# Layer 2 of a four-layer graph kernel: x2 turned by VectorE in squares of 32, h in x2's place, a seventh stream buffer, and the last output block stored in two parts

## The chip, the cores and the metric

The kernel runs on one core of one Trainium2 chip. The metric is the device time of one execution in microseconds (us). The core has five engines that matter here: TensorE (PE, with its weight loads PEld), VectorE (DVE), ScalarE (ACT), GpSimd (POOL) and SyncE (SP), which issues most transfers. Each engine works through its own instructions in order and waits at semaphores for the others. The core's 16 DMA engines serve the queues of SP and of ACT.

## The reference

Four layers work on x (3327 nodes, 64 features) and one dense 3327 x 3327 adjacency matrix that is mostly zeros. Each layer adds its result to its input and normalises the rows.

```python
x = _layernorm(x + _L0_gnn_ref(t, x, adj))          # elementwise after the norm
x = _layernorm(x + _L1_gnn_ref(x, adj, att_W, att_b)) # attention over all pairs of nodes
x = _layernorm(x + _L2_gnn_ref(x, adj, W))          # two hops, below
x = _layernorm(x + _L3_gnn_ref(x, adj, weight, bias)) # ranked neighbours, weights 0.5**k

def _L2_gnn_ref(user_embs, adj, W):
    x = user_embs
    for k in range(2):
        agg = adj @ x
        x = tanh(concat([agg, x], axis=1) @ W[k])
    return x
```

The change is in layer 2 and in the very end of layer 3. Layer 2 is, per hop, `tanh(adj @ (x @ W_top) + x @ W_bottom)`: the kernel multiplies by W first and then by the matrix.

## The kernel before

**Data.** The nodes are padded to 3328, which are 26 blocks of 128. The host hands in the transposed matrix, so that block `jb` of it is a tile [128, 3328] of float32: 1664 KB, or 13 KB in each partition. Four blocks (`kept`, loaded in layer 1) and two more (`late`, loaded near its end) stay in on-chip memory through layer 2. Features of nodes are kept in two forms: by node (128 nodes in the partitions, 64 features in a row) and stacked (64 features of the lower half of the nodes and 64 of the upper half in the 128 partitions, 1664 columns).

**Layer 2.** The function `layers` begins with it. `x2`, by node, is layer 1's result; the last DVE instructions of layer 1 write it (L1556 to L1558). `hT` is x2 in stacked form. It lies in the tile that the code calls `x3` or `x2T`, and since x2 + layer 2's result is formed later in stacked form (`with_x2`), it has to stay. For each of the two hops `k`:

- `top(i)` makes x @ W_top by node in `hw` (the tile `lj`), 128 nodes at a time. For hop 0 layer 1's end has made it already (`begun_here` is true in this run), so hop 0 can start with the large products.
- `bottom(c)` adds x @ W_bottom of a quarter (chunk) `c` of 416 columns to the accumulator `acc[c]` and needs `hT`. The four accumulators lie in two PSUM tiles: chunks 0 and 2 share one, chunks 1 and 3 the other.
- `add(c, jb)` adds one block's product to a chunk, for both halves of the nodes. A block takes 16 matmul records at L403.
- `chunk_end(c)` adds the last kept blocks (`end`, two in hop 0, three in hop 1) to one chunk and applies tanh on ACT. The result goes to `nxt`.

Both hops go through all 26 blocks. Hop 0 uses the six kept blocks, four blocks that were loaded ahead into the pool `strm` (four buffers), and sixteen that are loaded in the loop: into `strm`, or into the pool `more` (two buffers). The blocks loaded last in hop 0, six of them, are still there when hop 1 begins; hop 1 uses them first, and loads the other 14. SP issues a load when the buffer's former block has been used by PE (L209).

`hT` is made while hop 0 runs: after the fourth and fifth block, `turned(i)` transposes 13 groups of 128 nodes on PE (L345) into PSUM, and ACT copies them out (L349). After the sixth block come the four `bottom` products (L394), and behind the copies a one-element tanh (`warm_t`, L486) whose only purpose is that ACT loads the table of tanh.

`nxt` comes from a pool `cols` with two buffers of 6.5 KB in each partition. The same pool gives `accT` in layer 3, the sums of one half of the nodes.

**Layer 3.** When both blocks of `more` that hop 1 loaded have been used, that pool is closed and the first masks of layer 3 are made in its place (`masks`, L337). Then the layer runs through the matrix in two halves of 1664 columns, with its own half-blocks `ah` streamed in (L335). The order of PE, ACT and DVE is written out by hand in `layers` (`manual_schedule`).

**The end.** `last_out` makes the second half's output. The sums are multiplied back to nodes in three parts (blocks 0 to 5, 6 to 9, 10 to 12), x3 is added, ACT squares, DVE sums, and `rsqrt_of` gives one over the root of the variance: a step on DVE (L542), Sqrt on ACT (L236), then a reciprocal, and one refining step in four DVE instructions (L239 to L243). Each part is multiplied by it (L824) and stored, in turn by SP, ACT and SP (L764). The last block has only 127 real nodes; ACT stores it by itself (L828). After that every engine branches to the program's closing block, in which SP waits for all transfers.

Of the kernel before, what the change touches and what calls it, by code (L numbers as in the profile page):

```python
# [10 lines left out]
F32 = mybir.dt.float32  # L11
# [3 lines left out]
AF = mybir.ActivationFunctionType  # L15
ALU = mybir.AluOpType
# [3 lines left out]
P = 128  # L20
N = 3327
NB = 26
NP = NB * P
D = 64
CW = 416
HALF = NP // 2
NBH = NB // 2
# [12 lines left out]
EARLY = 4  # L40
LATE = 2
UNDER_WAY = 4

LN_EPS = 1e-5
MIN_NORM = 1e-15
# [28 lines left out]
def kernel(  # L74
# [11 lines left out]
    nc = tc.nc  # L86

    const = ctx.enter_context(tc.tile_pool(name="const", bufs=1))
    small = ctx.enter_context(tc.tile_pool(name="small", bufs=2))
# [22 lines left out]
    )  # L112
    ones = const.tile([P, 1], F32, name="ones")
    nc.vector.memset(ones, 1.0)

    attw_dg = const.tile([P, 4], F32, name="attw_dg")
    nc.vector.memset(attw_dg, 0.0)
# [147 lines left out]
    def by_half(v):  # L265

        return v.rearrange("p (n h) d -> p n h d", h=2)
# [39 lines left out]

    @with_exitstack
    def layers(ctx, x2, x3, begun_here, kept, ready, ahead_ctx, strm):
        cols = ctx.enter_context(tc.tile_pool(name="cols", bufs=2, reuse_waits="tile"))  # L310

        more_ctx = ExitStack()
        more = more_ctx.enter_context(tc.tile_pool(name="more", bufs=2, reuse_waits="tile"))
        l3m = None
        in_order = ctx.enter_context(ExitStack())
        in_order.enter_context(tc.manual_schedule(engines={mybir.EngineType.PE}))
# [20 lines left out]
            nc.vector.tensor_scalar(mask[q], at, 0.0, None, ALU.not_equal)  # L337

        groups = fours

        def to_stack(ps, src, dst, g, n, copy, name):

# [34 lines left out]
        with tc.tile_pool(name="l2p", bufs=2, space=PSUM, reuse_waits="tile") as l2p:  # L377
            for k in range(2):
                hw = lj
                nxt = cols.tile([P, HALF], F32, tag="hT", name=f"hT_{k + 1}")  # L380
                begun = set()

                def turned(i):
                    to_stack(l2p, x2, hT, *groups[i], nc.scalar.copy, "x2")

                groups = fours if k else threes

                def top(i, copy=nc.vector.tensor_copy):
                    g, n = groups[i]
                    pn = node_products(l2p, hT, w2_dg[:, 2 * k, :], g, n, f"l2_{k}")  # L390
                    copy(by_half(hw)[:, g : g + n], pn)  # L391

                def bottom(c):
                    nc.tensor.matmul(  # L394
                        acc[c], w2_dg[:, 2 * k + 1, :], hT[:, c * CW : (c + 1) * CW],
                        start=c not in begun, stop=False, skip_group_check=True,
                    )
                    begun.add(c)

                def add(c, jb, last=False):  # L400
                    for h in range(2):
                        o = h * HALF + c * CW
                        nc.tensor.matmul(  # L403
                            acc[c][h * D : (h + 1) * D, :], hw[:, slot(jb), :],
                            blocks[jb][:, o : o + CW], start=c not in begun, stop=last,
                            skip_group_check=True,
                        )
                    begun.add(c)

                stay = list(kept)
                if k:
                    stay.sort(key=lambda jb: jb >= NB - EARLY)
                n_end = 3 if k else 2
                stay, end = stay[:-n_end], stay[-n_end:]
                others = [jb for jb in range(NB) if jb not in kept and jb not in ready]
                share = -(-len(others) // len(stay))
                order = list(ready)  # L420
                if k:

                    order, others, share = order + others[:5], others[5:], 3
                for i, jb in enumerate(stay):
                    order += [jb] + others[i * share : (i + 1) * share]
                blocks = {**ready, **kept}

                if k == 0 and not begun_here:
                    turned(0)
                    turned(1)  # L430
                    top(0, nc.scalar.copy)
                    turned(2)
                    top(1)
                    for c in range(CPH):
                        add(c, order[0])
                    turned(3)
                    top(2)
                    turned(4)
                    top(3)
                    for c in range(CPH):  # L440
                        add(c, order[1])
                    top(4)
                    for c in range(CPH):
                        bottom(c)

                    warm_t = small.tile([P, 1], F32, tag="warm", name="warm_t")
                    nc.scalar.activation(warm_t, ones, AF.Tanh)
                    order = order[2:]
                elif k:
                    top(0)  # L450
                    bottom(0)
                    bottom(1)
                    top(1)
                    bottom(2)
                    for c in range(CPH - 1):
                        add(c, order[0])
                    top(2)
                    bottom(CPH - 1)
                    add(CPH - 1, order[0])
                    top(3)  # L460
                    order = order[1:]
                seen, held = {}, {}
                for i, jb in enumerate(order):
                    if jb not in blocks:
                        if len(seen) % (UNDER_WAY + 2) < 2 and (k == 0 or len(seen) < 2):
                            blocks[jb] = held[jb] = block(more, jb, tag="bt", name=f"bt_l2_{k}_{jb}")
                        else:
                            blocks[jb] = block(strm, jb, tag="at", name=f"at_l2_{k}_{jb}")
                        seen[jb] = blocks[jb]
                    for c in range(CPH):  # L470
                        add(c, jb)
                    if k == 0 and begun_here:

                        if i == 3:
                            turned(0)
                            turned(1)
                        if i == 4:
                            turned(2)
                            turned(3)
                            turned(4)  # L480
                        if i == 5:
                            for c in range(CPH):
                                bottom(c)

                            warm_t = small.tile([P, 1], F32, tag="warm", name="warm_t")
                            nc.scalar.activation(warm_t, ones, AF.Tanh)  # L486
                    if k and jb in held and len(held) == 2:
                        for q in range(AHEAD + 3):
                            masks(q)
                def chunk_end(c):  # L490
                    for jb in end:
                        add(c, jb, jb == end[-1])
                    nc.scalar.activation(nxt[:, c * CW : (c + 1) * CW], acc[c], AF.Tanh)  # L493

                if k:
                    break
                for c in range(CPH):
                    chunk_end(c)

                last = sorted(list(seen)[-UNDER_WAY - 2 :], key=lambda jb: jb not in held)  # L500
                ready = {jb: seen[jb] for jb in last}
                hT = nxt

# [36 lines left out]
        def rsqrt_of(v, w):  # L540

            nc.vector.tensor_scalar(v, v, 1.0 / D, LN_EPS, ALU.mult, ALU.add)  # L542
            return rsqrt(v, "ln", w)

        def spread(v, n):
            return v.unsqueeze(2).to_broadcast([P, n, D])
# [184 lines left out]

        def sums_out(h):

            accT = cols.tile([P, HALF], F32, tag="hT", name=f"accT_{h}")
            to = [
                accT[:, 2 * c * CW : 2 * (c + 1) * CW].rearrange("p (e k) -> p e k", e=2)
                for c in range(2)
            ]
            nc.scalar.activation(to[0], acc[h, 0], AF.Identity, bias=b3_sb)
            nc.vector.tensor_scalar(to[1], acc[h, 1], b3_sb, None, ALU.add)  # L740
            return accT
# [54 lines left out]
        def last_out(h, accT):  # L796
# [20 lines left out]
            added(2)  # L817
            summed(1)
            summed(2)
            r = rsqrt_of(v, NBH)  # L820

            rows = N - h * HALF - (NBH - 1) * P
            for s, queue in zip(parts, (nc.sync, nc.scalar, nc.sync)):
                nc.vector.tensor_tensor(  # L824
                    hh[:, s], hh[:, s], spread(r[:, s], s.stop - s.start), ALU.mult
                )
                if store(queue, h, hh, s):
                    nc.scalar.dma_start(out[N - rows :], hh[:rows, NBH - 1])  # L828

        first_out = None  # L830
        with_step = [
# [993 lines left out]
```

## Time and profile before

| what | value |
|---|---|
| median of 3 runs | 562.38 us (562.27 to 563.3) |
| the profiled execution, device time | 562.28 us |
| its span in the profile | 560.5 us |
| mean granted TensorE clock | 0.987 |
| PE busy | 527.3 us, 94% of the span |
| DVE, ACT, POOL busy | 368.2, 278.1, 215.7 us |
| layer 1 ends, first block of layer 2 on PE | 241.86 us |
| first tanh of hop 0 on ACT | 316.56 us |
| first `top` of hop 1 on PE | 320.63 us |
| first tanh of hop 1 on ACT | 396.30 us |
| last instruction issued for the output (ACT's store of 127 rows) | 554.71 us, for 0.59 us |

The span is what the profiler sees between the first and the last instruction. The device time of the same execution is 1.8 us longer. The page's 40 slices give the engines' busy tenths and what the DMA moved:

```profile
PE   8989989999999999999999999998989999999992
DVE  6899999999999999791000011300478878787834
ACT  4899999999999998612000100000274333343311
DMA  8976766676766715699999149996609996789701
GB/s 305 353 273 205 234 209 204 222 233 199 238 205 223 235 32 222 272 425 425 425 426 424 43 148 417 425 425 291 244 8 343 342 303 227 237 258 358 274 2 36
```

A slice is 14 us. Layer 2 is slices 18 to 29. There PE is busy throughout, DVE and ACT hardly at all, and the DMA moves 425 GB/s, but for two slices in the middle and two at the end. The page's list of transfers gives their sizes and the median time from issue to landing:

```profile
at_l<-in_adjT SPq DMA_DIRECT2D x26, 1664.0 KB, 13.7
bt_l<-in_adjT SPq DMA_DIRECT2D x8, 1664.0 KB, 12.8
```

`at_l` are blocks in `strm`, `bt_l` blocks in `more`: 34 loads of layer 2, of which four are those loaded ahead.

### The profile page before, as it was taken

The page shows a single profiled execution, that of the slowest core. Times are in us where ns is not written, and L with a number is a line of the kernel's source. Part 1 is how long each engine was busy: PE and PEld are TensorE (multiplying, and loading weights), DVE is VectorE, ACT ScalarE, POOL GpSimd, SP SyncE. Part 2 cuts the span into 40 slices and gives each one's busy share as a digit, 9 for nine tenths or more (in the row PEclk, how much of TensorE's full clock was granted, in tenths as well). Part 3 has the DMA queues.
Part 4 walks back from the last instruction along what each step waited for, and adds up shares of the span by engine and source line. Part 5 has one row for each costly group of instructions (what it writes and reads, how often), then busy time and mean ns, then how long its engine had stood idle before and what let it go on. Part 6 is the DMA issues. An engine that isn't in the chain of part 4 may idle for free.

```text
span 560.5 us, 7513 instructions
## 1 busy us (share of the span) xinstructions
PE 527.3 (94%) x2854; PEld 226.6 (40%) x2854; DVE 368.2 (66%) x532; ACT 278.1 (50%) x328; POOL 215.7 (38%) x138
## 2 busy tenths in 40 slices
PE   8989989999999999999999999998989999999992
PEld 5522222222222222854444444443455555545542
DVE  6899999999999999791000011300478878787834
ACT  4899999999999998612000100000274333343311
POOL 3799999999999999200000000000011000000000
PEclk9899999999999999899999999999999999999997
DMA  8976766676766715699999149996609996789701
GB/s 305 353 273 205 234 209 204 222 233 199 238 205 223 235 32 222 272 425 425 425 426 424 43 148 417 425 425 291 244 8 343 342 303 227 237 258 358 274 2 36
DMA packets 34037, 145.27 MB, mean 259 GB/s; under 512 B 10285, under 2 KB 11975, under 8 KB 28871
## 3 DMA queue, kind: packets, MB, share of 16 engines
q1 hardware_dynamic: 31655, 144.11, 69.8%
q10 hardware_dynamic: 2336, 0.59, 0.5%
q8 instruction: 24, 0.39, 0.3%
q14 instruction: 22, 0.18, 0.1%
HBM read 143.23 MB, written 0.87 MB: 257 GB/s over the span
## 4 chain that ended last, share of the span: by engine, by line
PE 61%; DVE 20%; ACT 8%; DMA 6%; issue 3%; DVEq 0%
PE cnt L403 20%; PE pq L1075 12%; DVE v L1096 12%; PE cnt L513 11%; PE acc L709 6%; DMA at_l<-in_adjT 5%; ACT sg L1051 4%; PE acc L724 3%; ACT pq L1088 3%; DVE a L1087 2%; DVE w L526 1%; PE cnt L394 1%; DVE mask L337 1%; DMA x<-in_x 1%; PE pm L1367 1%
## 5 line engine op out<-in xcount | busy, mean ns | idle before, releaser
L1062 POOL TENSOR_TENSOR u<-sg,at 128x832 f32<-128x832 f32 x88 | 170.0, 1964 | 3.5 <-ACT sg L1051 3.0
L1075 PE MATMUL pq<-riT,ljT 64*128 64x416 f32 x416 | 100.2, 560 | 15.2 <-DVE v L1096 6.2
L1087 DVE SCALAR_TENSOR_TENSOR a<-pq,dl,u 128x832 f32<-128x832 f32 x104 | 111.9, 1077 | 2.9 <-PE pq L1075 2.8
L1088 ACT ACTIVATE pq<-pq,al,gas 128x832 f32<-128x832 f32 x104 | 105.0, 1011 | 15.1 <-DVE a L1087 14.2
L1096 DVE SCALAR_TENSOR_TENSOR v<-pq,a 128x832 f32<-128x832 f32 x104 | 105.7, 1016 | 1.1 <-ACT pq L1088 0.8
L1108 PE MATMUL acc<-v,xv 128*64 128x416 f32 x416 | 95.4, 537 | 0.1
L403 PE MATMUL cnt<-at_l,lj 128*64 128x416 f32 x480 | 86.1, 513 | 2.3 <-DMA at_l<-in_adjT 2.3
L1051 ACT ACTIVATE sg<-lb,rb 128x1664 f32<-128x1664 f32 (+1 forms) x53 | 87.3, 1647 | 0.1
L528 ACT ACTIVATE w<-cnt 128x832 int16<-128x832 f32 x55 | 47.3, 863 | 71.5 <-PE cnt L513 71.4
L640 POOL TENSOR_TENSOR s<-sq,s 128x384 bf16<-128x384 f32 (+1 forms) x4 | 4.1, 1028 | 200.3 <-ACT s L639 200.3
L493 ACT ACTIVATE hT<-cnt 128x416 f32<-128x416 f32 x8 | 4.1, 517 | 138.3 <-PE cnt L403 138.3
L1075 PEld LDWEIGHTS pq<-riT,ljT 64*128 64x128 f32 x416 | 31.5, 184 | 88.3 <-DVE v L1096 83.1
L526 DVE TENSOR_SCALAR w<-cnt 128x832 int16<-128x832 f32 x49 | 50.1, 1023 | 25.8 <-PE cnt L513 24.5
L403 PEld LDWEIGHTS cnt<-at_l,lj 128*64 128x64 f32 x480 | 34.1, 137 | 52.1 <-issue 47.3
L513 PE MATMUL cnt<-mask,tri 128*128 128x416 bf16 x208 | 53.5, 339 | 0.1
L709 PE MATMUL acc<-w,s 128*128 128x416 bf16 x208 | 52.6, 339 | 0.5 <-DVE hid L781 0.5
L513 PE MATMUL cnt<-mask,rest 128*128 128x416 bf16 x200 | 51.6, 340 | 1.2 <-ACT w L528 0.6
L391 DVE COPY lj<-pn_l 128x512 f32<-128x512 f32 (+1 forms) x4 | 2.4, 592 | 73.9 <-PE pn_l L355 73.9
L1108 PEld LDWEIGHTS acc<-v,xv 128*64 128x64 f32 x416 | 20.6, 134 | 61.0 <-issue 57.8
L337 DVE TENSOR_SCALAR mask<-ah 128x1664 bf16<-128x1664 f32 x42 | 43.4, 1034 | 0.0
L403 PE MATMUL cnt<-kept,lj 128*64 128x416 f32 x192 | 35.5, 514 | 0.0
L1062 POOL TENSOR_TENSOR u<-sg,kept 128x832 f32<-128x832 f32 x16 | 31.0, 1972 | 2.6 <-ACT sg L1051 2.6
(282 smaller groups left out, 403.7 us busy)
## 6 DMA issues: line engine op xcount, KB each, us to landing
at_l<-in_adjT SPq DMA_DIRECT2D x26, 1664.0 KB, 13.7
at<-in_adjT SPq DMA_DIRECT2D x44, 832.0 KB, 4.9
ah<-in_adjT SPq DMA_DIRECT2D x42, 832.0 KB, 6.3
bt_l<-in_adjT SPq DMA_DIRECT2D x8, 1664.0 KB, 12.8
kept<-in_adjT SPq DMA_DIRECT2D x6, 1664.0 KB, 8.7
lb<-lf_rows SPq DMA_DIRECT2D x2, 384.0 KB, 4.5
ljT<-ljT SPq DMA_DIRECT2D x4, 128.0 KB, 6.2
x<-in_x ACTq DMA_DIRECT2D x1, 416.0 KB, 5.5
```

What stands on the lines that cost most here:

```text
L337: nc.vector.tensor_scalar(mask[q], at, 0.0, None, ALU.not_equal)
L403: nc.tensor.matmul(acc[c][h * D : (h + 1) * D, :], hw[:, slot(jb), :], blocks[jb][:, o : o + CW], start=c not in begun, stop=last, skip_gr ...
L513: nc.tensor.matmul(cnt[c][:, e, :], mat, mask[q][:, of], start=start, stop=(mat is tri), skip_group_check=True,)
L526: nc.vector.tensor_scalar(w.bitcast(I16), cnt[c], 0.0, None, ALU.max)
L709: nc.tensor.matmul(acc[h, c][:, e, :], s12[:, slot(jb)].rearrange("p t d -> p (t d)"), ws[q, c][:, e, :], start=first, stop=last,)
L1051: nc.scalar.activation(sg[:, :, of], lbs[:, :, of], AF.Sigmoid, bias=rb[:, sl : sl + 1])
L1062: nc.gpsimd.tensor_tensor(u, sg[:, :, of], at[:, :, of], ALU.mult)
L1075: nc.tensor.matmul(pq[:, h, :], ljT[h != jb // NBH][rows, of], riT[rows, ch * CW : (ch + 1) * CW], start=True, stop=True,)
L1087: stt(a_s[t], pqs[t], dl[:, one], us.pop(t), op0=ALU.add, op1=ALU.mult)
L1088: nc.scalar.activation(pqs[t], pqs[t], AF.Square, bias=al[:, one], scale=gas[:, one])
L1096: stt(w, pqs.pop(t), CUBIC_REST, a_s.pop(t), op0=ALU.add, op1=ALU.mult)
L1108: nc.tensor.matmul(accs[cp, ci][h * D : (h + 1) * D, :], xv[:, slot(jb), :], w[:, h, :], start=(jb == orders[cp][0]), stop=(jb == orders[c ...
```

## The change

- `cols` is no pool any more, but the tile x2 under another shape. h of both hops and both `accT` are written there. x2 has been turned into `hT` by then.
- `more` has three buffers (`MORE = 3`). With the four of `strm` there are seven; the last seven blocks loaded in hop 0 stay for hop 1, and the masks start when the third block of `more` has been used in hop 1.
- `turned_by_squares` makes `hT` by 16 DVE transposes in squares of 32 x 32, each over 13 blocks of nodes (StreamTranspose of 32x13x32), before the loop of hop 0. PE's transposes and ACT's copies in that hop go. `bottom` and `warm_t` come after the ninth block instead of the sixth.
- In `last_out`, ACT takes the Sqrt with scale and bias from the summed squares themselves; `eps` is a small tile for the bias, set by POOL at the start. The refining step has one instruction fewer, and its factor -0.5 goes into the last product.
- The 127 rows of the last block are stored as 112 (ACT) and 15 (SP).

```diff
+MORE = 3
...
+    eps = const.tile([P, 1], F32, name="eps")
+    nc.gpsimd.memset(eps, LN_EPS)
...
     def layers(ctx, x2, x3, begun_here, kept, ready, ahead_ctx, strm):
-        cols = ctx.enter_context(tc.tile_pool(name="cols", bufs=2, reuse_waits="tile"))
+
+        cols = x2.rearrange("p n d -> p (n d)")
 
         more_ctx = ExitStack()
-        more = more_ctx.enter_context(tc.tile_pool(name="more", bufs=2, reuse_waits="tile"))
+        more = more_ctx.enter_context(tc.tile_pool(name="more", bufs=MORE, reuse_waits="tile"))
...
+        def turned_by_squares(src, dst):
+
+            Q = 32
+            to = dst.rearrange("p (n k) -> p n k", k=P)
+            for h in range(2):
+                for f in range(D // Q):
+                    rows = slice(h * D + f * Q, h * D + (f + 1) * Q)
+                    for q in range(P // Q):
+                        nodes = slice(q * Q, (q + 1) * Q)
+                        nc.vector.transpose(
+                            out=to[rows, :, nodes],
+                            in_=by_half(src)[nodes, :, h, f * Q : (f + 1) * Q],
+                        )
...
-                nxt = cols.tile([P, HALF], F32, tag="hT", name=f"hT_{k + 1}")
+                nxt = cols
...
+                elif k == 0:
+                    turned_by_squares(x2, hT)
                 elif k:
...
-                        if len(seen) % (UNDER_WAY + 2) < 2 and (k == 0 or len(seen) < 2):
+                        if len(seen) % (UNDER_WAY + MORE) < MORE and (k == 0 or len(seen) < MORE):
...
-                        if i == 3:
-                            turned(0)
-                            turned(1)
-                        if i == 4:
-                            turned(2)
-                            turned(3)
-                            turned(4)
-                        if i == 5:
+                        if i == 8:
                             for c in range(CPH):
                                 bottom(c)
...
-                    if k and jb in held and len(held) == 2:
+                    if k and jb in held and len(held) == MORE:
...
-                last = sorted(list(seen)[-UNDER_WAY - 2 :], key=lambda jb: jb not in held)
+                last = sorted(list(seen)[-UNDER_WAY - MORE :], key=lambda jb: jb not in held)
...
-            accT = cols.tile([P, HALF], F32, tag="hT", name=f"accT_{h}")
+            accT = cols
...
-            r = rsqrt_of(v, NBH)
+
+            r0, r = (small.tile([P, NBH], F32, tag=f"last_{k}", name=f"last_{k}") for k in range(2))
+            nc.scalar.activation(r0, v, AF.Sqrt, bias=eps, scale=1.0 / D)
+            nc.vector.tensor_scalar(v, v, 1.0 / D, LN_EPS, ALU.mult, ALU.add)
+            nc.vector.reciprocal(r0, r0)
+            nc.vector.tensor_tensor(r, v, r0, ALU.mult)
+            nc.vector.tensor_tensor(r, r, r0, ALU.mult)
+            nc.vector.scalar_tensor_tensor(r, r, -3.0, r0, op0=ALU.add, op1=ALU.mult)
...
-                nc.vector.tensor_tensor(
-                    hh[:, s], hh[:, s], spread(r[:, s], s.stop - s.start), ALU.mult
+                nc.vector.scalar_tensor_tensor(
+                    hh[:, s], hh[:, s], -0.5, spread(r[:, s], s.stop - s.start),
+                    op0=ALU.mult, op1=ALU.mult,
                 )
                 if store(queue, h, hh, s):
-                    nc.scalar.dma_start(out[N - rows :], hh[:rows, NBH - 1])
+                    most = rows // 16 * 16
+                    nc.scalar.dma_start(out[N - rows : N - rows + most], hh[:most, NBH - 1])
+                    nc.sync.dma_start(out[N - rows + most :], hh[most:rows, NBH - 1])
```

## The prediction

> **What bounds the kernel now.** I read the chain of waits first, then the windows of layer 2, then the timeline of single engines where the chain changes hands. Line numbers are those of the kernel before; "us" are microseconds from the start of the span.
>
> The chain's shares say TensorE (PE) almost everywhere, so an edit on another engine counts only where PE, or the end, waits for it:
>
> ```profile
> PE 61%; DVE 20%; ACT 8%; DMA 6%; issue 3%; DVEq 0%
> ```
>
> The chain in order of time, cut to layer 2, shows two transfers in it, one at the end of each hop (k=0 and k=1):
>
> ```profile
> 264.31 30.90 PE cnt L403 x176
> 295.23 16.83 DMA at_l<-in_adjT
> 312.10 8.60 PE cnt L403 x48
> ...
> 330.08 47.66 PE cnt L403 x272
> 377.76 13.34 DMA at_l<-in_adjT
> 391.15 7.20 PE cnt L403 x40
> ```
>
> The windows (PE, PEld, DVE, ACT, POOL busy, granted clock, DMA share, GB/s) tell how far each of the two is from its bound:
>
> ```profile
> 228.00:300.00 72.00, 71.76 (x432) 37.87 (x432) 23.48 (x92) 11.41 (x30) 0.00 (x0) 0.98 1.00 417
> 300.00:309.00 9.00, 9.00 (x56) 3.66 (x54) 0.00 (x0) 0.00 (x0) 0.00 (x0) 1.00 1.00 423
> 309.00:312.00 3.00, 2.95 (x18) 0.99 (x14) 0.00 (x0) 0.00 (x0) 0.00 (x0) 1.00 0.25 107
> 312.00:328.00 16.00, 15.90 (x91) 8.02 (x92) 1.38 (x2) 2.07 (x4) 0.00 (x0) 1.00 0.00 1
> ...
> 388.00:391.00 3.00, 1.00 (x6) 0.14 (x2) 0.00 (x0) 0.00 (x0) 0.00 (x0) 1.00 0.07 31
> ...
> 556.80:559.20 2.40, 0.00 (x0) 0.00 (x0) 0.00 (x0) 0.00 (x0) 0.00 (x0) 0.50 0.10 24
> ```
>
> Hop 0: the DMA is full from 228 to 309 while PE is full too; both end together. Then 16 us without a transfer, because every stream buffer holds a block that hop 1 uses again. Hop 1: PE stands still before its last streamed block. The end: 2.4 us at 0.10 of the engines, a store that crawls. PE and ACT at these places:
>
> ```profile
> 253.18 0.87 PE L345 MATMUL pt_x<-ident,x 128*128 128x128 f32 x6
> 256.93 0.87 PE L345 MATMUL pt_x<-ident,x 128*128 128x128 f32 x6
> 391.15 3.01 PE L403 MATMUL cnt<-at_l,lj 128*64 128x416 f32 x16 [2.15 <-DMA at_l<-in_adjT]
> ```
>
> ```profile
> 258.70 1.28 ACT L486 ACT_TABLE_LOAD   x1
> 316.56 0.52 ACT L493 ACTIVATE hT<-cnt 128x416 f32<-128x416 f32 x1 [56.37 <-PE cnt L403]
> ```
>
> **What the Trainium skill says.** "DMA: Bandwidth & Descriptors", section "Why a DMA increments its semaphore by 16 and not by 1": a transfer from SP or ACT uses the largest number of engines up to 16 that divides the row count; 127 partitions get one engine. The trace agrees (0.10 of 16 engines above). "Vector Engine (DVE) Microarchitecture Reference", section 3.8: the 32x32 transpose sustains one element per cycle per lane; no run here shows one yet. "ScalarE: Activation LUTs", section "What ACT_TABLE_LOAD costs": 1283 ns, plus about 1380 ns of drain; the trace shows the 1.28 us and the next ACTIVATE right behind it (258.70 to 259.99), so I use 1.30. "Runtime: NRT & Kernel Launch", section "Instruction fetch mechanics": a taken branch breaks the prefetch. The trace agrees: ACT's last store is issued by 555.30 and its first record behind the branch, a drain, stands at 558.5.
>
> **1. x2 turned by DVE.** Removed: 13 PE transposes and 5 ACT copies. In PE's time that is 253.99-253.18=0.81 plus 258.31-256.93=1.38, so 2.19 us. Added: 16 StreamTranspose of 32x13x32, in DVE's queue right behind the last product of x2 (ends 254.17). The nearest row is L573, 128x416 f32 in 0.59 us; at the page's rate the transpose moves 416 elements per lane as well, so I take 0.5 to 0.6 us: 16 x 0.55 = 8.8, done at 263. PE needs it for the four "bottom" products, now behind nine blocks: 253.18 + 5 x 2.80 = 267.2. DVE has nothing else until 321.8, so nothing is queued behind. Cover is 4 us; it holds up to 0.8 us an instruction. At the low bound (0.45) nothing changes; at a high bound of 1.0 (array filled, then drained: two passes) the bottoms start at 270.2; from there 2.99 + 14 blocks x 2.80 lead to 312.4 for the last streamed block, 0.3 late, since the waits counted next absorb the rest.
>
> The 2.19 us are not gained. The last streamed block of hop 0 lands at 312.10 and the blocks land 4.0 us apart (1.704 MB at 425 GB/s), a stream that starts at 227.62 as before and carries the same 20 blocks. PE's new schedule with 2.80 us a block (264.24 to 308.98 is 16 blocks) wants block 15 at 295.3, which lands at 296.1; wants block 18 at 307.3, lands 308.1; wants the last at 310.9, lands 312.1. So PE waits 0.8+0.8+1.2 instead of computing: gain 0. DMA order and issue don't hurt: the third new buffer's first load waits for near_end's small DVE and ACT results (240.1) and sits behind two issues at 242.07, well before the queue runs dry at 248.
>
> **2. Tanh table.** With the copies gone, `warm_t` has nothing ahead of it on ACT and the order listing puts it at the start of layer 1, before the sigmoids, where ACT idles for 1.7 us (13.46 to 15.16): free, but useless as a warm-up. The load now stands directly before hop 0's first tanh and behind an event wait for that chunk's matmuls. So tanh 0 ends at 316.56+1.30+0.52=318.38 instead of 317.08. PE's matmuls for chunk 2 share chunk 0's accumulator tile and wait for tanh 0; they started at 317.74. Loss: 318.38+0.05-317.74=0.69, with restart 0.75. Tanh 1 (318.9) is needed at 319.8, so it costs once. Bounds: 0 if the load runs ahead of the wait, 2.1 if the page's drain comes on top.
>
> **3. Seventh buffer, h in x2's place.** Two `cols` tiles (2 x 6.5 KB a partition) become the third `more` block. Seven blocks stay for hop 1, so 13 are loaded instead of 14. Hop 1's first load again waits for the first reused block, 0.75 later; one block fewer is 4.0 earlier: the last lands at 391.15+0.75-4.0=387.9. PE, without stalls, wants its last streamed block (again behind 22 others) at 389.0+0.75=389.75. The 2.15 us stall goes, with 1.85 to spare; what is late next is nothing before layer 3, where all moves together. Checked on the way: each later load's buffer (four in rotation) comes free 0.4 us or more before the stream needs it. `ah`, the masks (now after the third held block, about 356, wanted at 403) and both accT in x2's place wait for things long done. Layer 2 net: -2.15+0.75=-1.40.
>
> **4. The end.** Root: before, from the variance at 551.74 to the first product at 553.30, 1.56. After, Sqrt with scale and bias runs first (0.25), `tensor_scalar` waits for it since it overwrites v (0.10 to the next issue), reciprocal 0.27, three steps of 0.21: 1.25. Gain 0.31. The products change from tensor_tensor to scalar_tensor_tensor: L613 shows 0.55 for the same 384 elements, no change. Store: 127 rows become 112 (16 engines) and 15. SP then sets the end, not the store. SP's last issue ends at 554.99 and the trace's records of its closing waits begin at 558.33, come every 0.065, then stop until 559.50 for the 127 rows; its drain is at 559.62. After: 554.99-0.31+0.45 for one more issue (stores took 0.39 to 0.59) =555.13, +3.34, + 8 x 0.065 = 558.99. The 15 rows, issued at 554.7, have landed by about 557.2. Gain 0.63 with the root in it. Bounds: 0.3 and 1.1. The `eps` memset on POOL lies in an idle stretch until 5.62: 0.
>
> **Sum.** -1.40-0.63=-2.03 on a profiled execution of 562.28 (span 560.5): 560.25. The median of the runs, 562.38, is 0.1 higher; I say 560.2.
>
> **Rivals.** (a) The table load costs nothing: 562.28-2.15-0.63=559.5. For it: ACT idles 56 us before. Against: the order listing has the wait first. (b) The last transfer's lag grows (it landed 1.5 us later than the 4.0 us step from its forerunner) or hop 1's start slips, so the stall stays: 562.28+0.75-0.63=562.4, no change. Against: 1.85 us of slack. (c) Slower: the squares. Their end, 254.2+16T, may slip to 269.9 (312.1-42.2) before the last streamed block is late, so T decides from 0.98 us and adds 16(T-0.98). At 1.5 us: 560.2+8.3=568.5. For it: no record of this instruction, strided 32-wide rows, float32. Against: the page's rate.
>
> **Numbers.** Forecast 0.64, (a) 0.14, (b) with its halfway forms 0.12, (c) 0.10. A measurement here tells 0.2% (1.1 us) from no change, so half of (b) counts as faster and half as the same. The range 559.0 to 561.4 leaves out (c) and the worse half of (b). Faster 0.83, same 0.08, slower 0.09.
>
> **What would show it.** Hop 0: PE's last streamed block still starts at 312.1, with stalls of about 0.8, 0.8 and 1.2 before it; a table load at 316.6 and chunk 2 at 318.4. Hop 1: no DMA stall, last streamed block at 389.7. End: DMA done by 557.5. Wrong if the squares end after 270, if block 19 of hop 0 starts earlier than 311.5, or if a stall remains at the end of hop 1.

## The result: 0.23% slower

| | before | changed |
|---|---|---|
| median of 20 runs each | 561.99 us (560.17 to 563.32) | 563.56 us (561.7 to 564.27) |
| ratio to before, 95% interval | | 1.0023 (1.0013 to 1.0032) |
| the profiled execution, device time (span) | 562.28 us (560.5) | 563.86 us (562.1) |

I forecast 560.2 us, a gain of about 2. It became a loss: 1.3 us by the ratio, 1.6 by the two medians.

### The profile after

The shares of the chain of waits are those of before within a point:

```profile
PE 62%; DVE 20%; ACT 8%; DMA 5%; issue 3%; DVEq 0%; ACTq 0%
```

The windows of the changed kernel (PE, PEld, DVE, ACT, POOL busy, granted clock, DMA share, GB/s):

```profile
309.00:312.00 3.00, 2.40 (x14) 0.92 (x14) 0.00 (x0) 0.00 (x0) 0.00 (x0) 1.00 0.78 328
312.00:328.00 16.00, 14.50 (x82) 6.63 (x80) 1.38 (x2) 3.24 (x5) 0.00 (x0) 1.00 0.01 5
388.00:391.00 3.00, 3.00 (x20) 1.26 (x18) 0.00 (x0) 0.00 (x0) 0.00 (x0) 1.00 0.61 252
556.80:559.20 2.40, 0.00 (x0) 0.00 (x0) 0.00 (x0) 0.00 (x0) 0.00 (x0) 0.50 0.05 11
559.20:562.00 2.80, 0.00 (x0) 0.00 (x0) 0.00 (x0) 0.00 (x0) 0.00 (x0) 0.50 0.03 9
```

Layer 2 looks as forecast: PE waits a little at the end of hop 0, and no longer in hop 1 (3.00 busy of 3.00 where it was 1.00). The last row is the news: after 559.2 no engine computes, hardly a byte moves, and still the kernel runs on to 562.1. The timeline of TensorE, VectorE and ScalarE at the places of steps 1 to 3:

```profile
256.13 10.11 DVE L354 STREAM_TRANSPOSE xc<-x 32x416 f32<-32x416 f32 x16
297.88 3.01 PE L421 MATMUL cnt<-at_l,lj 128*64 128x416 f32 x16 [0.45 <-DMA at_l<-in_adjT]
309.87 3.02 PE L421 MATMUL cnt<-bt_l,lj 128*64 128x416 f32 x16 [0.60 <-DMA bt_l<-in_adjT]
313.84 3.02 PE L421 MATMUL cnt<-bt_l,lj 128*64 128x416 f32 x16 [0.96 <-DMA bt_l<-in_adjT]
318.33 1.28 ACT L506 ACT_TABLE_LOAD   x1 [75.87 <-PE cnt L421]
320.20 3.01 PE L421 MATMUL cnt<-kept,lj 128*64 128x416 f32 x16 [0.55 <-ACT x L506]
```

The squares take 10.11/16 = 0.63 us each. Three DMA waits (0.45, 0.60, 0.96) stand in hop 0, the table load stands behind PE's products, and PE loses 0.55 us to it.

Now the end. When the stores are issued, SP runs a closing sequence of 13 instructions, all on the program's last line; the first eight are waits. The first two lines are those waits in the kernel before, in the windows 558.0 to 558.75 and 559.45 to 559.72; the next two are the changed kernel's, 558.0 to 558.95 and 560.80 to 561.34. Between the two windows of each kernel SP has no record. Columns: count, shortest/median/longest ns, first and last start.

```profile
L1821 SPq EVENT_SEMAPHORE  x6: 28/28/28, 558.3 to 558.7; - x6
L1821 SPq EVENT_SEMAPHORE  x2: 28/28/28, 559.5 to 559.6; - x2
```

```profile
L1844 SPq EVENT_SEMAPHORE  x2: 27/28/28, 558.8 to 558.9; - x2
L1844 SPq EVENT_SEMAPHORE  x6: 28/28/28, 560.9 to 561.2; - x6
```

Before: six waits 0.065 apart, then a pause that ends when the store of 127 rows lands (559.48 in the transfer records). Changed: two waits, then 2.0 us of nothing, then six in a row. The last landing was at 559.06, and no transfer arrives at 560.88, so this is no wait for data. The trace has packets of 8192 bytes at 559.34 and 560.05 in the queue that brings instructions. That alone proves little, since the kernel before, without the stop, has two such packets as well (558.93 and 559.15).

### One table for all profiles

Three stretches matter. "Start": ACT's third table load, which ends layer 1's attention. "Layer 2": from there to the first product of layer 3 on PE (`both`, L580 before). "End": from the last `accT` bias on ACT to the end of the span. Layer 3 between them takes 148.0 us in every profile.

| kernel | start | layer 2 | end |
|---|---|---|---|
| before | 234.55 | 163.73 | 14.17 |
| before_again | 234.30 | 162.46 | 13.83 |
| changed | 236.48 | 161.84 | 15.83 |
| after_again | 235.07 | 161.76 | 15.58 |
| before_pad | 236.51 | 162.59 | 15.23 |
| end_only | 236.35 | 162.43 | 13.56 |
| l2_only | 235.97 | 161.53 | 15.35 |
| after_pad2 | 236.22 | 161.65 | 13.91 |
| old_store | 236.33 | 161.80 | 13.77 |
| six_buffers | 234.92 | 162.53 | 13.54 |
| pe_turn | 235.03 | 160.89 | 13.55 |
| warm_tied | 234.83 | 160.91 | 13.73 |
| joined | 234.81 | 161.55 | 13.20 |
| joined_warm | 236.56 | 160.97 | 13.46 |

Of the 14 starts, seven lie at 234.3 to 235.1 and seven at 236.0 to 236.6. In the second group TensorE's clock stood at half for 6.8 us (12.4 to 19.8 in the records), in the first for 3.4. Before_pad runs exactly before's instructions there and is in the second group, after_again in the first, so a late start is nothing that only the changed kernel has, and the 1.9 us by which its first profile started later are not counted as its work. Whether the change makes late starts more frequent was not tested.

### The profile page after: what moved, and what is told of

The parts are those of the page before. It is cut to its first block, busy times and chain, and to the rows that moved or that the text cites. A ratio compares the mean times of both kernels' runs of the same rounds, so it can differ in the third digit from the quotient of the medians.

```text
span 562.1 us, 7490 instructions
## 1 busy us (share of the span) xinstructions
PE 526.6 (94%) x2841; PEld 226.2 (40%) x2841; DVE 377.5 (67%) x547; ACT 276.3 (49%) x323; POOL 215.6 (38%) x139
## 4 chain that ended last, share of the span: by engine, by line
PE 62%; DVE 20%; ACT 8%; DMA 5%; issue 3%; DVEq 0%; ACTq 0%
PE cnt L421 22%; PE pq L1098 12%; DVE v L1119 12%; PE cnt L526 11%; PE acc L722 6%; DMA bt_l<-in_adjT 4%; ACT sg L1074 4%; PE acc L737 3%; ACT pq L1111 3%; DVE a L1110 2%; DVE w L539 1%; PE cnt L412 1%; DVE mask L341 1%; DMA x<-in_x 1%; PE x_w L1434 1%
## 5 line engine op out<-in xcount | busy, mean ns | idle before, releaser
L421 PE MATMUL cnt<-at_l,lj 128*64 128x416 f32 x416 | 74.6, 513 | 0.5 <-DMA at_l<-in_adjT 0.5
L421 PEld LDWEIGHTS cnt<-at_l,lj 128*64 128x64 f32 x416 | 29.7, 137 | 43.2 <-issue 41.1
L506 ACT ACTIVATE x<-cnt 128x416 f32<-128x416 f32 x8 | 4.0, 516 | 79.1 <-PE cnt L421 79.0
L421 PE MATMUL cnt<-bt_l,lj 128*64 128x416 f32 x224 | 40.9, 514 | 1.6 <-DMA bt_l<-in_adjT 1.6
L506 ACT ACT_TABLE_LOAD x1 | 1.3, 1283 | 75.9 <-PE cnt L421 75.9
```

What stands on the lines that cost most here:

```text
L421: nc.tensor.matmul(acc[c][h * D : (h + 1) * D, :], hw[:, slot(jb), :], blocks[jb][:, o : o + CW], start=c not in begun, stop=last, skip_gr ...
```

## Experiments

In the "Theory F" texts, F is instruction fetch, E the end's edits themselves, S a start made later by the change. Times are medians of 9 to 22 runs (one run each for the two repeats), ratios those to the kernel before on the same chip. The experiments ran on four chips, so between experiments the ratios compare better than the medians. Each experiment but before_pad, end_only and the repeats starts from the changed kernel.

### Where SP's closing sequence lies

The kernel has an If with two arms, of which one runs. I counted SP's instructions in each built program, from 0 and with both arms (this is not in the profile). The closing sequence of 13 begins at number 849 before and at 847 in the changed kernel; in both cases SP comes to it by the branch over the arm that does not run.

**after_pad2**: the changed kernel, its closing sequence moved to 850.

```diff
+                pad = small.tile([P, 1], F32, tag="pad", name="pad")
+                for _ in range(2):
+                    nc.sync.dma_start(pad[:D, :], b3.rearrange("(d o) -> d o", o=1))
```

> The changed kernel with two small DMAs (three SP instructions) added to the arm of the If that does not run. Theory F (instruction fetch): in the changed kernel SP's closing sequence of 13 instructions stood still for 2.0 us between its second and third wait (558.86 to 560.88) because its first two instructions lie in one fetched stretch of code and the other eleven in the next; the added instructions move the whole sequence into one stretch, so the gap goes, the closing waits follow one another at 0.065 us until the last store's landing (559.1), and the time falls by 1.6 us from 563.56 to about 561.9. Theory E (the end edits themselves are slower: SP's extra store and its later branch): nothing moves, 563.5.

560.9 us, ratio 0.9987 (0.9979 to 0.9995). Two DMAs that never run turn the loss into a gain: 1.0023 against 0.9987 is 0.36%, 2.0 us (2.7 by the medians), more than the 1.6 that I expected. SP's waits of this kernel, 557.9 to 558.64:

```profile
L1847 SPq EVENT_SEMAPHORE  x8: 28/28/28, 558.0 to 558.5; - x8
```

All eight in one run, no gap. Theory E falls: what runs is the same, and the position of the code alone decides. That the stop is a fetch of instructions (theory F) is the reading that foretold it; the trace has no record that ties the stop to one fetch.

Without the gap SP is no longer the last. Its second drain comes at 558.67, ScalarE's first closing record, a drain, only at 558.92, and all engines go on at 559.17:

```profile
L1847 SPq DRAIN  x3: 7/7/13, 558.6 to 559.3; - x3
L1847 ACTq DRAIN  x2: 8/44/81, 558.9 to 559.3; - x2
```

**before_pad**: the kernel before with the same lines, 119 instead of 2, in the same arm; the closing sequence then begins at 975 = 847 + 128.

> The kernel before, with a loop of 119 small DMAs (126 SP instructions) in the arm of the If that does not run, so that SP's closing sequence begins two instructions ahead of the end of a fetched stretch if such a stretch is 128 instructions, as in the changed kernel. Nothing that runs is altered. Theory F: a gap of 2.0 us after the second closing wait, SP done at about 560.7 in place of 559.7: 1.0 us slower, 563.0. Theories E and S: no change, 562.0.

563.59 us, ratio 1.0029 (1.0016 to 1.0041). Its closing waits, 558.9 to 559.2 and 561.05 to 561.5:

```profile
L1824 SPq EVENT_SEMAPHORE  x2: 28/28/28, 559.1 to 559.1; - x2
L1824 SPq EVENT_SEMAPHORE  x6: 28/28/28, 561.1 to 561.4; - x6
```

The gap of the changed kernel appears in the old one. It was expected to cost 1.0, and in the profile the end is 1.1 to 1.4 longer than before's; the ratio says 1.6 (0.9 to 2.3).

**end_only**: the kernel before with the new root and the split store, nothing else. Closing sequence at 851.

> The kernel before with the new end alone (the shorter root and the store in 112 and 15 rows); layer 2 as before. Theory F: SP's closing sequence lies in one stretch here, so the end gains 0.24 us from the root and about 0.4 from the store that lands earlier: 561.4, no gap of 2 us among SP's closing waits. Theory E: the end costs 1.65 us as in the profiled pair, 563.6. Theory S (the later start of layer 1's attention, +1.9 us in the profiled pair, is caused by the change): if the memset of eps is its cause the start shows here too, 563 to 563.5 under F; if not, the first layer-2 block stays near 241.9.

561.96 us, ratio 1.0002 (0.999 to 1.0015). No gap among the waits; the end is 0.3 to 0.6 shorter than before's two. The time does not show this gain (561.4 was expected), but its interval, -0.6 to +0.8 us, leaves room for it. E's loss of 1.65 us is excluded. The start was late, 236.35, as in before_pad without `eps`: a late start does not need the memset.

**l2_only**: the changed kernel with the old end. Closing sequence at 845.

> The changed kernel with the old end (old root, one store of 127 rows): layer 2's part alone. Layer 2 itself should be 1.9 us shorter than before (156.4 to 154.5) in every theory. Theory F: SP's closing sequence begins four instructions ahead of the end of a fetched stretch, so a gap of 2.0 us is expected between its fourth and fifth wait, which costs 1.2 us against before, since before waited until 559.5 for the store: 562.0 - 1.9 + 1.2 = 561.3 if the start of layer 1 is chance. Theory E: the old end is as good as before, 560.1. Theory S (the warming tanh in layer 1 or the moved code makes layer 1 end 1.5 to 1.9 us later): add that, 562.9 under F.

561.94 us, ratio 0.9999 (0.999 to 1.0008). Its closing waits, 557.2 to 557.72 and 559.70 to 560.0:

```profile
L1832 SPq EVENT_SEMAPHORE  x4: 28/28/28, 557.5 to 557.7; - x4
L1832 SPq EVENT_SEMAPHORE  x4: 28/28/28, 559.7 to 559.9; - x4
```

Four waits, gap of 2.0, four waits, as expected: 845 + 4 = 849. So layer 2's gain was eaten by the position of code that layer 2 doesn't touch. The time forecast, 561.3, was 0.6 too low; the expected layer 2 gain of 1.9 came from a profile pair that overstates it (see before_again).

The positions agree on one rule: the gap comes where instruction 849 or 977 is crossed soon after the branch (after 2, 2 and 4 instructions), and none comes where the sequence starts at 849, 850, 851, 856 or 861.

### Layer 2, part by part

The next kernels all have the closing sequence in one stretch, by the same lines in the arm that does not run (two DMAs; three in old_store, eight in the two joined kernels), so after_pad2 is what they are read against.

**warm_tied**: the warming tanh can't run ahead into layer 1.

```diff
-                            nc.scalar.activation(warm_t, ones, AF.Tanh)
+                            nc.scalar.activation(warm_t, hT[:, 0:1], AF.Tanh)
```

> As after_pad2, but the warming tanh reads h's first column, so that it can't run ahead into layer 1 and the tanh table is loaded in hop 0, under TensorE's work, as before. Theory P (TensorE's own waits are the path in layer 2): the wait of 0.55 us of chunk 2 on the tanh of chunk 0 goes and the time falls by as much against after_pad2, 560.9 to 560.3. Theory D (the loads of hop 1 set layer 2's end: in after_pad2 the last streamed block landed at 390.64 and was multiplied from about 391.0): only the 0.3 us of slack can be won, 560.6, and a wait for the last streamed block appears. If the table load cost nothing, 560.9.

560.43 us, ratio 0.9972 (0.9958 to 0.9986). ACT's timeline:

```profile
240.84 1.28 ACT L499 ACT_TABLE_LOAD   x1
262.73 0.20 ACT L499 ACTIVATE warm_t<-xc 128x1 f32<-128x1 f32 x1 [20.60 <-DVE xc L354]
316.54 0.52 ACT L506 ACTIVATE x<-cnt 128x416 f32<-128x416 f32 x1 [53.60 <-PE cnt L421]
```

The table load is back under TensorE's work, PE's wait for the tanh is gone and layer 2 is 0.74 shorter (161.65 to 160.91). Theory P; the loads of hop 1 did not come in the way. Against after_pad2 the time fell by 0.5 in medians and 0.8 in ratios.

**pe_turn**: x2 turned by TensorE and ScalarE as before, all else as in after_pad2.

```diff
-                elif k == 0:
-                    turned_by_squares(x2, hT)
...
-                        if i == 8:
+                        if i == 3:
+                            turned(0)
+                            turned(1)
+                        if i == 4:
+                            turned(2)
+                            turned(3)
+                            turned(4)
+                        if i == 5:
```

> As after_pad2, but x2 is turned by TensorE with ScalarE's copies, at the same places as before, and the warming tanh stands after them. Prediction's step 1: hop 0 is bound by its loads, TensorE's 2.19 us of transposes fill time that it would otherwise wait, so hop 0's last streamed block is multiplied at the same distance from layer 2's start; and the table load comes back to hop 0, -0.5: together 560.4 to 560.9. Rival (the turns were on the path): about 2 us slower, 562.9.

560.65 us, ratio 0.9973 (0.9963 to 0.9982). Here the table load is early too, so the fair partner is warm_tied: layer 2 takes 160.89 against 160.91. It makes no difference which engine turns x2.

**six_buffers**: MORE = 2 in after_pad2.

> As after_pad2, but with six stream buffers (MORE = 2), so that hop 1 loads 14 blocks again; SP's closing sequence stays in one fetched stretch. My prediction's step 3 put the seventh buffer at the whole stall of 2.15 us that the profiled run of before showed; by it layer 2 gets 1.4 to 2.1 us longer and the time is 562.3 to 563.0. Rival: that stall was large because layer 1 ended early in that one run (234.6 us against 236 in the other five profiles); with the usual start it is 0.6 to 1.2 us, and the time is 561.5 to 562.1.

562.11 us, ratio 1.0011 (0.9998 to 1.0024), 1.2 us above after_pad2 by the medians; layer 2 is 0.9 longer. The stall of hop 1 is back on PE, smaller than in before:

```profile
390.32 3.01 PE L421 MATMUL cnt<-at_l,lj 128*64 128x416 f32 x16 [0.48 <-DMA at_l<-in_adjT]
```

Hop 1, from its first `top` to layer 3's first product, takes 75.9 here and 75.2 in every profile with seven buffers. The rival (0.6 to 1.2) is right on the size. Its reason, the late start, is not: this profile started at 234.92.

**before_again** and **after_again**: both kernels unaltered, one more profile each.

> The kernel before, unaltered, for a second profile. The start of layer 1's attention and the stall ahead of hop 1's last streamed block are asked for. If the stall belongs to the kernel, it is 2.15 us again; if it hangs on how early layer 1 ended (2.15 at 234.6, 1.24 and 0.64 at 236.4 to 236.5 in the two profiles of kernels with the same layer 2), it lies between 0.6 and 2.2 with the start, and a time of 562.28 is above the median 561.75 by chance.

> The changed kernel, unaltered, for a second profile. Theory F: SP stands still for 2.0 us after its second closing wait again. The start of layer 1's attention (236.5 in the first profile, 234.8 to 236.5 in the experiments) may come out early this time, with one half-clock stretch of 3.4 us in place of 6.8; then the time is 562.4 to 562.8, otherwise 563.7.

Before_again ran 560.32 us. Its start was even earlier than in the first profile (234.30), and PE's waits for loads in hop 1 were these two:

```profile
377.64 3.01 PE L403 MATMUL cnt<-at_l,lj 128*64 128x416 f32 x16 [0.49 <-DMA at_l<-in_adjT]
389.63 3.01 PE L403 MATMUL cnt<-at_l,lj 128*64 128x416 f32 x16 [0.59 <-DMA at_l<-in_adjT]
```

1.08 in all, not 2.15, and layer 2 1.27 us shorter than in the first profile. In the first, the sixteen parts of the last load were done between 387.79 and 391.10, 3.3 us apart; in this one between 387.26 and 389.58. One straggler of that execution had been read as the kernel's stall. The prediction's rival (b) had even noted that this load landed 1.5 us late. After_again ran 562.12 us with the gap between second and third wait (556.99 to 559.15) once more and an early start.

### What sets the end

**old_store**: after_pad2 with the 127 rows in one store.

> As after_pad2 (SP's closing sequence in one fetched stretch), but the last output block is stored in one part of 127 rows by ScalarE, as before. Prediction's step 4 gave the split 0.32 us: then this is 0.3 us slower than after_pad2, 561.2, with SP's seventh wait standing for the landing. Theory F2 (the fetch after SP's last branch sets the end once the store is short, and the split makes SP's branch 0.6 us later): the end is as long, 13.5 to 13.9 us from the last bias to the span's end, and the time is within 0.2 us of after_pad2.

561.31 us, ratio 0.9985 (0.9974 to 0.9996), against 0.9987 with the split. The end takes 13.77 against 13.91. The traces speak for F2, that the split buys nothing: with one store, SP's branch comes at 554.62, with two at 555.31, 8.49 and 9.46 us after the last bias. The fetch begins that much later, and what the landing gives the fetch takes. With one store a wait stands for the landing (558.32 to 558.64, landing at 558.62), and yet SP's second drain comes 12.76 us after the last bias, with two stores 12.82. In both profiles ScalarE's drain comes later still (559.05 and 558.92). The times cannot decide it: the median is near the 561.2 that the prediction's step 4 asks for, the ratio is that of after_pad2 within 0.1 us, as F2 has it, and the ratios' intervals are 0.4 to 0.6 us either way.

**joined**: the last product goes to x2's place, and the stores stand after both arms. The lines in the idle arm are left out here.

```diff
-                    hh[:, s], hh[:, s], -0.5, spread(r[:, s], s.stop - s.start),
+                    x2[:, s], hh[:, s], -0.5, spread(r[:, s], s.stop - s.start),
...
                 layers(x2, xc, False, *blocks)
+
+        rows = N - HALF - (NBH - 1) * P
+        most = rows // 16 * 16
+        for lo, hi, queue in ((0, 6, nc.sync), (6, 10, nc.scalar), (10, NBH - 1, nc.sync)):
+            queue.dma_start(
+                out[HALF + lo * P : HALF + hi * P].rearrange("(c p) d -> p c d", p=P), x2[:, lo:hi]
+            )
+        nc.scalar.dma_start(out[N - rows : N - rows + most], x2[:most, NBH - 1])
+        nc.sync.dma_start(out[N - rows + most :], x2[most:rows, NBH - 1])
```

> As the changed kernel, but the last product is written to x2's place and the last stores stand after the If, so that SP and ScalarE take the branch over the other arm before the stores, not after them. SP's closing sequence lies with its stores in one fetched stretch. Theory F (after a branch over the arm that does not run an engine stands for about 3 us while its code is fetched, and this sets the end): the end is then set by the stores' landings, about 3.3 us after the last is issued, and SP closes at 558 in place of 558.7: 0.5 to 1 us less than after_pad2, 560.0 to 560.4. Rival (the stores' landings set the end in both, or the second branch costs a fetch of its own): no gain, 560.9 or more.

560.23 us, ratio 0.9972 (0.9961 to 0.9983), 0.7 to 0.8 us below after_pad2. SP branches over the other arm at 523 us, long before the stores. SP's issues and its closing waits in this kernel:

```profile
551.78 1.03 SPq L1819 DMA_DIRECT2D out<-x  x2
552.88 0.48 SPq L1823 DMA_DIRECT2D out<-x  x1
```

```profile
L1851 SPq EVENT_SEMAPHORE  x8: 27/28/28, 556.2 to 556.7; - x8
```

The program still has a branch behind the stores. What it costs does not show: SP's first closing wait stands at 556.23, right behind the last landing at 556.22 (in joined_warm 557.64 and 557.62). ScalarE is no longer late either, its drain comes at 553.51. So the landings now set the end, as theory F had it. The gain in time is as expected; the end is 0.7 shorter than in after_pad2, but only 0.3 to 0.5 shorter than in the other four profiles with the split store and no gap.

**joined_warm**: both remedies.

> The two remedies together: the warming tanh tied to h's first column and the last stores behind the If, SP's closing sequence in one fetched stretch. If the two costs are separate (table load 0.5 us in layer 2, branch fetch 0.8 us at the end), the ratio to before is about 0.996 and the time 559.5. If both only uncover the same next limit, it stays at the 560.3 of each alone.

559.03 us, ratio 0.9951 (0.9936 to 0.9966), 2.7 us below before, more than with either remedy alone (0.9972): the two costs are separate, and this version beats both kernels.

## Why the prediction was wrong

**Step 4, the end: the step that failed.** It took over SP's closing records of before, a fetch behind the branch and then a wait every 0.065, and had the eighth wait over by 558.99. That wait stood at 561.22. The term at fault is one that was put at nothing without a reason: that the closing sequence follows the branch in one piece, wherever it lies. In the changed kernel it began two instructions ahead of a stretch's end, and a second stop of 2.0 us stood among the waits. The change has one executed SP instruction fewer and one fewer in the arm that does not run; that shift of two is the whole cause of the gap. By the ratios of the changed kernel and after_pad2 it costs 2.0 us of the 3.3 by which I was wrong. I had cited the Trainium skill, "Runtime: NRT & Kernel Launch", section "Instruction fetch mechanics", for the broken prefetch, and stopped there; the same section speaks of refills block by block and calls the crossing mostly hidden. Here, right after a branch, SP stood for 2.0 us.

Three smaller terms were off as well. The issues took longer: the last ended at 555.59, 0.46 after the forecast, because SP's last two took 0.65 each. The 15 rows landed at 559.06, not at 557.2. And "SP then sets the end" leaves out ScalarE, whose own wait behind the branch lasted 4.1 us here (3.2 before): in after_pad2 it, and not SP, is last. Without the gap the end takes 13.5 to 13.9 in place of 14.17 and 13.83, a gain of some 0.3, not 0.63. The root's part was right in kind and 0.06 too large: 1.31 us from the variance (551.75) to the first product (553.06), down from 1.56.

**Step 3, the seventh buffer: right mechanism, wrong size.** The stall went. But -2.15 was one execution's straggling load; in before_again, before_pad and end_only PE's waits for loads in hop 1 add up to 1.08, 1.24 and 0.91, and hop 1 as a whole takes 76.5 to 76.7 there against 75.2 with seven buffers, so the buffer is worth 1.3 to 1.5. Why it is worth only 0.7 in six_buffers, one profile, was not traced. Layer 2 gained 0.8 us in the usual run (162.5 to 161.7), not 1.40.

**Step 2, the table load: right.** 0.75 forecast, 0.55 of PE's wait in the profile, 0.74 of layer 2 in warm_tied. The places were as told: load behind the chunk's products, chunk 2 waiting. The Trainium skill, "ScalarE: Activation LUTs", section "What ACT_TABLE_LOAD costs", puts a drain on top of the load; it is not in the trace: the tanh starts 0.02 us behind it (319.61, 319.63).

**Step 1, the squares: right.** The gain was 0, because hop 0 waits for its loads (0.45 + 0.60 + 0.96 where I had 0.8 + 0.8 + 1.2). The squares came every 0.63 us, above my 0.55, under the 0.8 that the cover allows; rival (c) never came near.

**The rivals.** None named the true one. The slower case looked for a slow instruction in layer 2; the loss lay in code position, at a place that I had looked at record by record. Of the 3.3 us, 2.0 are the gap, 0.6 the seventh buffer and 0.3 the rest of the end; the last 0.4 lies within the ratio's interval and stays open. Late starts may be in it: 14 of the changed kernel's 20 runs have a mean clock of 0.984 or less (its late profile showed 0.982, its early one 0.985).

## What to carry to other kernels

When a kernel ends behind an If, count where the closing instructions lie, and put padding into the arm that does not run, or the last stores behind the If, before judging a change of half a per cent; otherwise a shift of two instructions is taken for the change. A stall that one profile shows is worth only what a second profile confirms, above all a wait for the last of several transfers. An early warm-up of a table belongs where something holds it back: give it an operand of the stage that it is meant for.

## What the runs showed of the hardware

- In the twelve profiles with the stores inside the If, SP stood for 2.7 to 3.4 us behind the taken branch, ACT for 3.0 to 4.2. Crossing instruction 849 or 977 just behind it stopped SP for 1.9 to 2.1 us more, in four profiles of four. The two lie 128 instructions apart, and the packets of instructions that arrive at the end are of 8192 bytes (another queue brought some of 16384 before). That the stretch is 128 and not a divisor of it is not shown.
- TensorE's half clock early on lasted 3.4 or 6.8 us and moved layer 1's end by 1.5 us. In after_pad2 the runs fall apart by it: 11 with a mean clock of 0.986 or more average 560.43 us, 11 with 0.984 or less 561.68. In the kernel before the same cut parts 30 and 11 of 47 runs by only 0.45 us (561.57 and 562.02), and the six between, at 0.985, average 562.81, so the mean clock is a blurred sign. What decides the length was not tested.
- The 32x13x32 float32 transpose on VectorE took 0.60 us, one every 0.63 us, 1.5 ns an element of a lane.
